# Nineteen table loads split between a GpSimd gather of 120 rows and a ScalarE load of 8, with short gathers between them

## The chip, the cores and the metric

The kernel runs on one core of one Trainium2 chip. The metric is device time in microseconds of one execution; lower is better. A core has TensorE (PE, its weight loads shown apart as PEld), VectorE (DVE), ScalarE (ACT), GpSimd (POOL) and SyncE (SP), which only issues transfers here. Transfers between HBM and the core's memory are carried out by 16 DMA engines; SP, ScalarE and GpSimd each put transfers in a queue of their own, and all queues are served by the same 16 engines.

## The reference

A table of N = 100001 items with D = 128 numbers each, 1024 sequences of T = 50 item numbers, and a spiking unit per sequence and dimension:

```python
e = emb[seq]                                  # 1024 x 50 x 128, row 0 of emb is zero
uF = cumsum(e, axis=1) / min(t, lengths)
y = (uF - mean) * rsqrt(var + BN_EPS) * gamma + beta     # mean, var over the sequences
# scan over t: v += (x - v) / 2; spike = v >= 1; v -= spike
uF_out = spikes.mean(axis=0)                  # 1024 x 128
scores = uF_out @ emb.T                       # 1024 x 100001
```

The output is 1024 x 100001 numbers of 4 bytes, 409.6 MB. The table is 51.2 MB.

## The kernel before, in words

**First stage** (to about 500 us). For each of 50 time steps GpSimd gathers 1024 rows of the table in eight indirect transfers of 128 rows (L208, one short in eight steps, in which SP loads 128 single rows instead, L229). TensorE transposes and sums them, VectorE and ScalarE do the statistics and the spiking step. Meanwhile the first 40 of 98 parts of the table are loaded by SP.

**Second stage.** The table is cut in 98 parts of 1024 rows. A part is loaded as 128 partitions of 8 rows, 4 KB each. The 98 parts are worked off in column groups c of `WIDTHS` parts: four of 2, four of 3, thirteen of 6. Before a group is needed, each of its parts is prepared (`prepare`, L149): TensorE transposes it in eight pieces (L137), ScalarE copies the result into one half of a pair, VectorE the remainder into the other (L153, L154). Then for each of 8 blocks n of 128 output rows (sequences) and each part q of the group, TensorE multiplies (`product`, L161), and ScalarE and VectorE in turn evict the 128 x 1024 result into the block's buffer `o` (L553, L555). When a block's parts are all in, SP stores it (`store`, L170): 128 rows of 24 KB for a group of six, 3 MB. From c = 8 on three `o` buffers take turns, so a block's first eviction waits until the store of three blocks before has landed, on all DMA engines that carry it.

**Loads in the second stage.** Parts 40 to 97 are fetched from c = 8 on, three parts at a time, after the blocks n = 1 and n = 4 of a group (end of the loop over blocks, `fetch(r, k, to_fetch, GROUP // 2)`, L575). `fetch` (L104) issues from ScalarE's queue for these parts: one transfer of 128 partitions x 3 parts x 4 KB. There are 19 of these; the last call fetches what is left, 84 rows of 4 KB and a row of 512 B. Two buffers `rows` of six parts alternate; a part's place is free when its transposes are done. The order of instructions is the order of the program, engine by engine; nothing reorders it.

GpSimd has nothing to do in the second stage, and the indirect gathers of the first stage are its last transfers.

Of the kernel before, what the change touches and what calls it, by code (L numbers as in the profile page):

```python
# [12 lines left out]
F32 = mybir.dt.float32  # L13
BF16 = mybir.dt.bfloat16
F32R = mybir.dt.float32r
I32 = mybir.dt.int32
U32 = mybir.dt.uint32
# [4 lines left out]
P = 128  # L22
BN_EPS = 1e-5
V_TH = 1.0
HALF = 1024
KQ = HALF // P
# [8 lines left out]

BY_SYNC = (11, 17, 22, 28, 33, 38, 43, 48)
AT_ONCE = 32

WIDTHS = 4 * [2] + 4 * [3] + 13 * [6]
NARROW, MIDDLE = 4, 8  # L40
# [3 lines left out]
def rec_kernel(  # L44
# [9 lines left out]
    nc = tc.nc  # L54
    B, T = seq.shape
    N, D = table.shape
# [7 lines left out]
    const = ctx.enter_context(tc.tile_pool(name="const", bufs=1))  # L64
# [9 lines left out]
    held_rows = const.tile([P, BANK], F32, tag="countB", name="held_rows")  # L74
    ids = const.tile([P, B - BANK - P], F32, tag="countC", name="ids")
    ident = const.tile([P, P], F32, tag="ident", name="ident")

# [11 lines left out]
    def size(q):  # L91
        return min(HALF, N - q * HALF)
# [4 lines left out]
    def group(g):  # L97
        at = g if g < AHEAD else AHEAD - 2 + g % 2
        r = rowp.tile([P, GROUP, HALF], F32, tag=f"rows{at}", name=f"rows_{g}")
        for k in range(GROUP):  # L100
            rows[g * GROUP + SHIFT + k if g else k + ASIDE * (k >= TWICE)] = r[:, k, :]
        return r

    def fetch(r, k, q, n):  # L104

        engine = nc.sync if q < held else nc.scalar
        n = min(n, parts - q)
        whole = n - (size(q + n - 1) < HALF)
        if whole:
            engine.dma_start(  # L110
                out=r[:, k : k + whole, :],
                in_=table[q * HALF : (q + whole) * HALF, :].rearrange("(q p k) d -> p q (k d)", p=P, k=KQ),
            )
        if whole < n:
            full, rest = divmod(size(parts - 1), KQ)
            c1 = (parts - 1) * HALF
            r = r[:, k + whole, :]
            if rest:
                at = full - full % 32
                nc.vector.memset(r[at : at + 32, :], 0.0)  # L120
                engine.dma_start(
                    out=r[full : full + 1, : rest * D],
                    in_=table[c1 + full * KQ : N, :].rearrange("(o k) d -> o (k d)", o=1),
                )
            if full:
                engine.dma_start(
                    out=r[:full, :],
                    in_=table[c1 : c1 + full * KQ, :].rearrange("(p k) d -> p (k d)", k=KQ),
                )
# [43 lines left out]
    with ExitStack() as ph:  # L173
# [16 lines left out]
        nc.sync.dma_start(out=gb[:, 1:2], in_=beta.rearrange("(d o) -> d o", o=1))  # L190
        first = group(0)
        fetch(first, 0, 0, TWICE)
        spare = asidep.tile([P, ASIDE, HALF], F32, tag="aside", name="spare")
        for k in range(ASIDE):
            rows[TWICE + k] = spare[:, k, :]
        fetch(spare, 0, TWICE, ASIDE)
        fetch(first, TWICE, SHIFT, GROUP - TWICE)
        for g in range(1, AHEAD):
            fetch(group(g), 0, g * GROUP + SHIFT, GROUP)
# [17 lines left out]
        starts = ids[:T, :P].bitcast(I32)  # L217
        regs = [nc.sync.alloc_register(f"row{k}") for k in range(AT_ONCE)]
        singles = {}

        def fetch_singles(i):
            t = BY_SYNC[i]
            rows_of = held_rows[:, i % (BANK // P) * P :][:, :P]
            singles[t] = rows_of
            for p0 in range(0, P, AT_ONCE):
                nc.sync.load(regs, starts[t : t + 1, p0 : p0 + AT_ONCE])
                for k, reg in enumerate(regs):
# [90 lines left out]
        def over(t, v):  # L318

            d = lp.tile([P, B], BF16, tag="d", name=f"d_{t}")  # L320
            nc.scalar.activation(d, v, AF.Identity, bias=less)  # L321
            return d
# [7 lines left out]
        whole = slice(0, B)  # L330
# [13 lines left out]
        for t in range(T):  # L344
# [29 lines left out]
            r = sp.tile([P, 1], F32, tag="r", name=f"r_{t}")  # L374
# [14 lines left out]
            q = sp.tile([P, 1], F32, tag="q", name=f"q_{t}")  # L389
# [20 lines left out]
            if not last:  # L410
# [12 lines left out]
                d = over(t, v)  # L423
# [3 lines left out]
                if t in (T - 8, T - 6):  # L427
                    q = (t - T + 8) // 2
                    pair(q)
                    prepare(q, vp.tile([P, HALF], F32, tag="v0", name=f"pt_{q}"))  # L430
                    if q == TWICE - 1:
                        for k in range(TWICE):
                            rows[GROUP + ASIDE + k] = first[:, k, :]
                        nc.sync.dma_start(
                            out=first[:, :TWICE, :],
                            in_=table[(GROUP + ASIDE) * HALF : (GROUP + SHIFT) * HALF, :].rearrange(
                                "(q p k) d -> p q (k d)", p=P, k=KQ
                            ),
# [41 lines left out]

    psum = ctx.enter_context(
        tc.tile_pool(name="psum", bufs=4, space=bass.MemoryType.PSUM, reuse_waits="tile")
    )
# [12 lines left out]
    for c, W in enumerate(WIDTHS):  # L498
# [38 lines left out]
        for n, q in blockwise:  # L537
            if n not in os:
                pool, tag, most = turns[blocks % len(turns)]
# [30 lines left out]
            if n in (1, 4) and c >= MIDDLE and to_fetch < parts:  # L570
                g, k = divmod(to_fetch - SHIFT, GROUP)
                if k or to_split >= (g - 1) * GROUP + SHIFT:
                    if k == 0:
                        r = group(g)
# [23 lines left out]
```

## Time and profile before

| what | value |
|---|---|
| median of 3 runs | 1562.74 us (1562.43 to 1562.77) |
| profiled execution, its own time | 1562.34 us |
| its span, first to last instruction | 1560.6 us |
| busy: PE, DVE, ACT, POOL | 1124.4, 949.3, 674.1, 372.8 us |
| written to HBM, read from HBM | 409.60 MB, 77.69 MB |
| DMA queue q1 (SP): packets, MB, share of 16 engines | 32944, 431.39, 65.8% |
| DMA queue q10 (ScalarE) | 7700, 30.23, 4.8% |
| DMA queue q0 (GpSimd) | 12544, 25.72, 6.2% |

How to read it: the page cuts the span in 40 slices of 39 us and gives each engine's busy share in tenths; the line DMA is the mean busy share of the 16 DMA engines. A window `A:B` gives, for a stretch of the span, the busy time of each engine with its instructions in brackets, then the granted TensorE clock, the mean busy share of the 16 DMA engines (0.06 is one engine of sixteen) and the GB/s that they moved. A packet is booked with its whole size at its place, so that shares of full stretches come out up to 1% over 1.00. In lists of waits, "A <- B" says that A's engine stood idle until B.

### The profile page before, as it was taken

The page shows a single profiled execution, that of the slowest core. Times are in us where ns is not written, and L with a number is a line of the kernel's source. Part 1 is how long each engine was busy: PE and PEld are TensorE (multiplying, and loading weights), DVE is VectorE, ACT ScalarE, POOL GpSimd, SP SyncE. Part 2 cuts the span into 40 slices and gives each one's busy share as a digit, 9 for nine tenths or more (in the row PEclk, how much of TensorE's full clock was granted, in tenths as well). Part 3 has the DMA queues.
Part 4 walks back from the last instruction along what each step waited for, and adds up shares of the span by engine and source line. Part 5 has one row for each costly group of instructions (what it writes and reads, how often), then busy time and mean ns, then how long its engine had stood idle before and what let it go on. Part 6 is the DMA issues. An engine that isn't in the chain of part 4 may idle for free.

```text
span 1560.6 us, 14364 instructions
## 1 busy us (share of the span) xinstructions
PE 1124.4 (72%) x4465; PEld 802.4 (51%) x4465; DVE 949.3 (61%) x1128; ACT 674.1 (43%) x698; POOL 372.8 (24%) x398
## 2 busy tenths in 40 slices
PE   4444444444445989989878888788887878888884
PEld 2211211111133777768666666666666656666663
DVE  5777777777778665667555555455555445555552
ACT  2333333333344555555444444444444444444442
POOL 7777777777775000000000000000000000000000
PEclk9999999999996999999999999989999999999997
DMA  9722222222223999999999999999999999999998
GB/s 346 270 54 54 54 55 54 54 54 54 54 55 106 402 407 417 420 413 405 426 427 427 420 427 424 429 408 416 426 428 427 418 425 403 433 416 426 429 386 364
DMA packets 53265, 488.25 MB, mean 313 GB/s; under 512 B 10991, under 2 KB 12272, under 8 KB 32068
## 3 DMA queue, kind: packets, MB, share of 16 engines
q1 hardware_dynamic: 32944, 431.39, 65.8%
q0 software_dynamic: 12544, 25.72, 6.2%
q10 hardware_dynamic: 7700, 30.23, 4.8%
q8 instruction: 35, 0.57, 0.1%
q14 instruction: 42, 0.34, 0.1%
HBM read 77.69 MB, written 409.60 MB: 312 GB/s over the span
## 4 chain that ended last, share of the span: by engine, by line
DMA 46%; POOL 20%; PE 14%; issue 10%; DVE 4%; ACT 4%; ACTq 0%; POOLq 0%; SPq 0%; DVEq 0%
DMA scores<-o 44%; POOL e L208 20%; PE po L161 13%; DVE o L553 3%; ACT o L555 3%; DMA e<-in_L_rec_emb_table,idx 2%; DVE pairs L154 1%; ACT pairs L153 1%; PE pt L137 0%; ACT hi L153 0%; PE pre L351 0%; DVE lo L154 0%; PE warm L337 0%; DMA idx<-in_r_seq 0%; ACTq L555 0%
## 5 line engine op out<-in xcount | busy, mean ns | idle before, releaser
L553 DVE TENSOR_SCALAR o<-po 128x1024 f32<-128x1024 f32 (+1 forms) x390 | 466.7, 1214 | 324.8 <-DMA scores<-o 184.5
L555 ACT ACTIVATE o<-po 128x1024 f32<-128x1024 f32 x392 | 392.9, 1025 | 498.4 <-DMA scores<-o 367.9
L208 POOL DMA_INDIRECT e<-in_L_rec_emb_table,idx x392 | 372.1, 949 | 121.5 <-issue 116.5
L161 PE MATMUL po<-pairs,countB 128*128 128x512 f32 (+1 forms) x1120 | 292.9, 408 | 59.1 <-ACT o L555 59.1
L351 PE MATMUL pre<-ident,e 128*128 128x128 f32 x392 | 171.9, 461 | 216.0 <-DMA e<-in_L_rec_emb_table,idx 214.7
L161 PE MATMUL po<-pairs,countC 128*128 128x512 f32 (+1 forms) x840 | 239.9, 433 | 58.1 <-ACT o L555 51.2
L161 PEld LDWEIGHTS po<-pairs,countB 128*128 128x128 f32 x1120 | 211.7, 194 | 120.6 <-ACT o L555 78.1
L351 PEld LDWEIGHTS pre<-ident,e 128*128 128x128 f32 x392 | 72.2, 185 | 318.6 <-DMA e<-in_L_rec_emb_table,idx 317.8
L161 PEld LDWEIGHTS po<-pairs,countC 128*128 128x128 f32 x840 | 169.1, 209 | 110.2 <-ACT o L555 62.5
L154 DVE TENSOR_TENSOR pairs<-pt,pairs 128x1024 fp32r<-128x1024 f32 x70 | 85.3, 1218 | 96.3 <-ACT pairs L153 96.2
L362 DVE SCALAR_TENSOR_TENSOR uF<-rlen,pre 128x512 f32<-128x512 f32 x100 | 68.3, 683 | 97.8 <-PE pre L351 97.7
L137 PE MATMUL pt<-ident,rows 128*128 128x128 f32 (+1 forms) x768 | 105.2, 282 | 10.0 <-DVE rows L134 4.9
L137 PEld LDWEIGHTS pt<-ident,rows 128*128 128x128 f32 (+1 forms) x768 | 94.7, 147 | 27.2 <-issue 10.8
L375 ACT ACTIVATE r<-mv,eps 128x1 f32<-128x1 f32 x50 | 14.8, 295 | 209.8 <-DVE mv L371 209.8
L309 PE MATMUL pre<-zT,ls 128*128 128x512 f32 x100 | 77.6, 778 | 26.2 <-DVE uF L362 22.3
L161 PE MATMUL po<-hi,countB 128*128 128x512 f32 x208 | 84.9, 408 | 13.4 <-ACT o L555 11.8
L153 ACT CAST pairs<-pt 128x1024 fp32r<-128x1024 f32 x70 | 70.1, 1014 | 41.3 <-PE pt L137 41.3
L161 PE MATMUL po<-lo,countB 128*128 128x512 f32 x208 | 83.0, 399 | 0.0
L321 ACT ACTIVATE d<-v,less 128x1024 bf16<-128x1024 f32 x49 | 54.5, 1113 | 65.4 <-DVE v L408 62.3
L161 PE MATMUL po<-hi,countC 128*128 128x512 f32 x156 | 67.7, 434 | 13.6 <-ACT o L555 12.4
L405 ACT ACTIVATE v<-uF,hgb,a 128x1024 f32<-128x1024 f32 x49 | 59.2, 1208 | 30.6 <-DVE a L401 30.6
L363 DVE BATCH_NORM_STATS2 bs<-uF 128x6 f32<-128x512 f32 x100 | 69.4, 694 | 3.4
(94 smaller groups left out, 858.5 us busy)
## 6 DMA issues: line engine op xcount, KB each, us to landing
scores<-o SPq DMA_DIRECT2D x96, 3072.0 KB
scores<-o SPq DMA_DIRECT2D x32, 1536.0 KB
scores<-o SPq DMA_DIRECT2D x29, 1024.0 KB
rows<-in_L_rec_emb_table ACTq DMA_DIRECT2D x19, 1536.0 KB
scores<-o SPq DMA_DIRECT2D x8, 2896.5 KB
held_rows<-in_L_rec_emb_table SPq DMA_DIRECT2D x1024, 0.5 KB
rows<-in_L_rec_emb_table SPq DMA_DIRECT2D x5, 3072.0 KB
e<-in_L_rec_emb_table,idx POOLq DMA_INDIRECT x392, 2.6
```

The lines of the kernel that those rows point to most:

```text
L137: nc.tensor.transpose(pt[:, k0 : k0 + pw], r[:pw, k0 : k0 + D], ident[:pw, :pw])
L153: nc.scalar.copy(vh, vp)
L154: nc.vector.tensor_tensor(vl, vp, vh.bitcast(F32), ALU.subtract)
L161: nc.tensor.matmul(po[:, :kw], lhsT=counts[n], rhs=part[:, k0 : k0 + kw], start=j == 0, stop=j == 1,)
L208: nc.gpsimd.indirect_dma_start(out=es[t][:, n * P : (n + 1) * P], out_offset=None, in_=table, in_offset=bass.IndirectOffsetOnAxis(ap=idx[: ...
L309: nc.tensor.matmul(pre[h], lhsT=l, rhs=zT[:, h * BANK : (h + 1) * BANK], start=t == 0, stop=False, skip_group_check=True,)
L351: nc.tensor.matmul(pre[h][:, k : k + P], lhsT=singles[t] if h * BANK + k + P == B and t in singles else e[:, h * BANK + k : h * BANK + k + P],
L362: nc.vector.scalar_tensor_tensor(uF[:, cs], rlen[:, cs], 1.0 / (t + 1), pre[h], ALU.max, ALU.mult)
L363: nc.vector.bn_stats(bs[:, h, :], uF[:, cs])
L405: nc.scalar.activation(vt, uF[:, cs], AF.Identity, bias=hgb[:, 1:2], scale=a)
L553: nc.vector.tensor_scalar_mul(o[:, h0 : h0 + hw], po[:, :hw], 1.0 / T)
L555: nc.scalar.mul(o[:, h0 : h0 + hw], po[:, :hw], 1.0 / T)
```

## The change

Of each of the 19 three-part loads, the third part (parts 42, 45, ... 96) is no longer in ScalarE's transfer, which now takes 128 partitions x 2 parts. The third part comes in two transfers: GpSimd gathers its first 120 rows of 4 KB (partitions 0 to 119) by an indirect transfer whose row numbers stand in a small table `picks`, made once by an `iota`; ScalarE loads its last 8 rows (partitions 120 to 127) by a plain transfer. After each such gather GpSimd issues a short one, `turn_by(17)`: 17 elements of 8 bytes into a tile that nothing reads. Before the second stage a single `turn_by(5)` gathers 5 such elements. The bytes of the table that arrive, and all arithmetic, are the same.

```diff
+SPARED = 120
+PICKED = range(42, 97, 3)
+TURN = 17
...
+    runs = table[: N // KQ * KQ, :].rearrange("(n k) d -> n (k d)", k=KQ)
+
+    def turn_by(m):
+        nc.gpsimd.indirect_dma_start(
+            out=turned_by[:m, :],
+            out_offset=None,
+            in_=table.rearrange("n (k d) -> (n k) d", d=2),
+            in_offset=bass.IndirectOffsetOnAxis(ap=picks[:m, 0:1].bitcast(U32), axis=0),
+        )
+
+    def pick(r, q, engine):
+        j = PICKED.index(q)
+        nc.gpsimd.indirect_dma_start(
+            out=r[:SPARED, :],
+            out_offset=None,
+            in_=runs,
+            in_offset=bass.IndirectOffsetOnAxis(ap=picks[:SPARED, j : j + 1].bitcast(U32), axis=0),
+        )
+        engine.dma_start(out=r[SPARED:, :], in_=runs[q * P + SPARED : (q + 1) * P, :])
+        turn_by(TURN)
+
     def fetch(r, k, q, n):
 
         engine = nc.sync if q < held else nc.scalar
         n = min(n, parts - q)
         whole = n - (size(q + n - 1) < HALF)
-        if whole:
+        wide = whole - (whole == n and q + whole - 1 in PICKED)
+        if wide:
             engine.dma_start(
-                out=r[:, k : k + whole, :],
-                in_=table[q * HALF : (q + whole) * HALF, :].rearrange("(q p k) d -> p q (k d)", p=P, k=KQ),
+                out=r[:, k : k + wide, :],
+                in_=table[q * HALF : (q + wide) * HALF, :].rearrange("(q p k) d -> p q (k d)", p=P, k=KQ),
             )
+        if wide < whole:
+            pick(r[:, k + wide, :], q + wide, engine)
...
+    nc.gpsimd.iota(picks, pattern=[[PICKED.step * P, len(PICKED)]], base=PICKED.start * P, channel_multiplier=1)
+    turn_by(5)
```

More of the change, by code (lines that the diff above doesn't have):

```diff
@@ L76, in rec_kernel @@
     ident = const.tile([P, P], F32, tag="ident", name="ident")
+    picks = const.tile([P, len(PICKED)], I32, tag="picks", name="picks")
+    turned_by = const.tile([TURN, 2], F32, tag="turned_by", name="turned_by")
     parts = -(-N // HALF)
```

## The prediction

> **What bounds the kernel now.** I read the page's parts 2, 3 and 6 first, then windows over the stage of stores, then what waits in it.
>
> ```profile
> PE   4444444444445989989878888788887878888884
> DMA  9722222222223999999999999999999999999998
> ...
> q1 hardware_dynamic: 32944, 431.39, 65.8%
> q0 software_dynamic: 12544, 25.72, 6.2%
> q10 hardware_dynamic: 7700, 30.23, 4.8%
> ...
> rows<-in_L_rec_emb_table ACTq DMA_DIRECT2D x19, 1536.0 KB
> ```
>
> From slice 13 on (about 500 us) the 16 DMA engines are full while TensorE is not. q1 carries the stores, q10 ScalarE's loads, q0 GpSimd's gathers, which all lie in the first stage. So the second stage is priced in time of DMA engines. The windows below cut it at the places where the DMA share falls (columns after the engines' busy times: granted clock, DMA share, GB/s).
>
> ```profile
> 795.50:888.50 93.00, 73.26 (x321) 57.32 (x322) 48.60 (x41) 41.27 (x42) 0.00 (x0) 0.93 1.01 429
> 888.50:891.50 3.00, 3.00 (x14) 2.47 (x13) 2.02 (x2) 1.03 (x1) 0.00 (x0) 0.94 0.65 276
> 891.50:1022.80 131.30, 108.96 (x471) 85.58 (x470) 69.92 (x60) 58.69 (x59) 0.00 (x0) 0.92 1.01 427
> 1022.80:1025.80 3.00, 3.00 (x15) 2.47 (x14) 2.39 (x2) 1.32 (x2) 0.00 (x0) 1.00 0.48 205
> 1025.80:1090.30 64.50, 52.41 (x228) 41.03 (x227) 33.57 (x29) 28.43 (x29) 0.00 (x0) 0.92 1.01 430
> 1090.30:1093.30 3.00, 3.00 (x15) 2.45 (x14) 2.19 (x2) 1.08 (x2) 0.00 (x0) 1.00 0.48 205
> 1093.30:1224.50 131.20, 109.33 (x472) 86.08 (x471) 70.29 (x60) 58.44 (x59) 0.00 (x0) 0.92 1.01 427
> 1224.50:1227.50 3.00, 3.00 (x15) 2.49 (x14) 1.96 (x2) 1.80 (x2) 0.00 (x0) 1.00 0.78 330
> 1227.50:1291.50 64.00, 51.14 (x222) 39.84 (x221) 33.45 (x28) 27.06 (x29) 0.00 (x0) 0.92 1.01 427
> 1291.50:1295.50 4.00, 4.00 (x18) 3.23 (x18) 2.33 (x2) 2.22 (x3) 0.00 (x0) 0.98 0.41 172
> 1295.50:1487.40 191.90, 160.01 (x703) 125.47 (x703) 106.04 (x90) 86.86 (x88) 0.00 (x0) 0.93 1.01 426
> 1487.40:1492.40 5.00, 5.00 (x19) 4.06 (x18) 2.17 (x3) 2.05 (x2) 0.00 (x0) 0.78 0.30 121
> 1492.40:1554.60 62.20, 42.22 (x181) 33.22 (x179) 25.16 (x24) 22.94 (x23) 0.00 (x0) 0.89 1.00 425
> 1554.60:1559.20 4.60, 0.00 (x0) 0.00 (x0) 0.00 (x0) 0.00 (x0) 0.00 (x0) 0.50 0.09 35
> ```
>
> Six short stops and a tail, and between them full engines. The stops lose 3.0x0.35 + 3.0x0.52 + 3.0x0.52 + 3.0x0.22 + 4.0x0.59 + 5.0x0.70 = 10.7 us of all 16 engines, the tail 4.6x0.91 = 4.2 us. Who still works in them?
>
> ```profile
> 1489.95:1491.40 1.45, 1.45 (x8) 1.17 (x7) 0.96 (x1) 0.71 (x1) 0.00 (x0) 1.00 0.04 17
> 1555.40:1556.30 0.90, 0.00 (x0) 0.00 (x0) 0.00 (x0) 0.00 (x0) 0.00 (x0) 0.50 0.12 51
> 1556.50:1559.10 2.60, 0.00 (x0) 0.00 (x0) 0.00 (x0) 0.00 (x0) 0.00 (x0) 0.50 0.06 27
> ```
>
> A share of 0.06 at 27 GB/s is one engine of sixteen at its full pace (q1: 431.39 MB in 65.8% of 16 x 1560.6 us is 26 GB/s an engine). So one engine is last by 4.4 us at the end, and at most one works in the middle of a stop. That it is the same engine throughout is my reading; the views do not name engines. It fits what the consumers wait for: a buffer is free when the last engine has landed its rows.
>
> ```profile
> 1477.87 18.30 SPq L170 DMA_DIRECT2D scores<-o  x3
> 1480.91 1.02 ACT L555 ACTIVATE o<-po 128x1024 f32<-128x1024 f32 x1 [4.21 <-DMA scores<-o]
> ...
> ACT o L555 <- DMA scores<-o: 281.2, 83, 6.4
> ```
>
> ScalarE waits 281.2 us of 765 for landings. Before the stop of 1487 it got its buffer only at 1480.9, and the block that it then evicted reached the queue too late for fifteen engines. On this reading the late engine never rests and sets the stage; the others stand idle 10.7x16/15 = 11.4 us in the stops and 4.2x16/15 = 4.5 us at the end: **15.9 us**, the most that moving work off it can return.
>
> **The change, part by part.** *Which engines.* What a transfer of few rows does must be inferred.
>
> ```profile
> DMA packets 307, 4.67 MB, mean 425 GB/s; under 512 B 46, under 2 KB 47, under 8 KB 131
> ...
> q10 hardware_dynamic: 100, 0.34, 7.7%
> ```
>
> This is 1443 to 1454 us, the last load: 84 rows of 4 KB and one of 512 B. The 19 whole loads take the other 7600 packets, 400 each: 384 rows and 16 completions. The last one's 100 packets are 85 rows and so 15 completions: one for the single row, 14 for the 84. So 84 rows went to 14 engines, the greatest number up to 16 that divides 84. If gathers divide alike (in the trace they have 128 rows only: 12544/392 = 32 packets, 16 of them data), 120 rows go to 15 engines of 8 rows, 17 to one, 5 to five, and ScalarE's 8 to eight. If each gather starts where the one before ended, 15 + 1 = 16 brings the turn back, so the same engine is left out nineteen times. [...]
>
> *Price of a row.* q10: 4.8% of 16 x 1560.6 us over 30.23 MB gives 0.162 us for 4 KB. The spared engine loses 19x8x0.162 = 24.7 us. If it is one of the eight that take the last rows it gets 3.1 us back; the seven others of the eight get +3.1 us each.
>
> *Gathered rows against loaded ones.* The filled stretch 0 to 70 us has both:
>
> ```profile
> q1 hardware_dynamic: 5750, 20.21, 77.4%
> q0 software_dynamic: 1632, 3.35, 13.6%
> ```
>
> 866.9 us for 20.21 MB is 0.176 us per 4 KB on q1; 152.3 us for 3.35 MB is 0.186 on q0, 6% more. Over the whole page q0 has 0.247, most of it from a stage whose engines are nearly empty. For 152 rows an engine the surplus is 0.01x152 = 1.5 us (bounds: 0, and (0.247-0.162)x152 = 12.9). I take 1.5, since the second stage is full as 0 to 70 is.
>
> *Short gathers.* Seventeen 8-byte elements on one engine, nineteen times. The nearest row is the single rows of the first stage, 100 to 430 us:
>
> ```profile
> q1 hardware_dynamic: 1640, 0.42, 0.5%
> ...
> held_rows<-in_L_rec_emb_table SPq DMA_DIRECT2D x822, 0.5 KB
> ```
>
> 26.4 us for 822 rows of 512 B, 0.032 us each; 17x0.032x19 = 10.3 us above, nothing below; I take half, 5.2 us, and on the engine that the turn ends on, the spared one.
>
> *Issue.* The order shows where they stand. On GpSimd after its last gather of the first stage (e is that stage's tile, rows the loaded one); before:
>
> ```order
> L208 DMA e_3277<-in_L_rec_emb_table,idx 128x128 x7
> L208 DMA e_3319<-in_L_rec_emb_table,idx 128x128 x8
> L594 UNCONDITIONAL_BRANCH
> L594 ISA
> ```
>
> and now:
>
> ```order
> L238 DMA e_3321<-in_L_rec_emb_table,idx 128x128 x8
> L513 IOTA picks 128x19
> L113 DMA turned_by<-in_L_rec_emb_table,picks 5x2
> L122 DMA rows_5442<-in_L_rec_emb_table,picks 120x1024
> L113 DMA turned_by<-in_L_rec_emb_table,picks 17x2
> L122 DMA rows_5442<-in_L_rec_emb_table,picks 120x1024
> ```
>
> GpSimd waits only for its own buffers. On ScalarE, at the first load, before:
>
> ```order
> L153 CAST pairs_4329<-pt_5427 128x1024
> L110 DMA rows_5438<-in_L_rec_emb_table 128x3x1024
> L555 ACTIVATE o_5_5440<-po_26_5441 128x1024
> ```
>
> and now:
>
> ```order
> L183 CAST pairs_4333<-pt_5431 128x1024
> L138 DMA rows_5442<-in_L_rec_emb_table 128x2x1024
> L128 DMA rows_5442<-in_L_rec_emb_table 8x1024
> L588 ACTIVATE o_5_5447<-po_26_5448 128x1024
> ```
>
> One load becomes two.
>
> ```profile
> L110 ACTq DMA_DIRECT2D rows<-in_L_rec_emb_table x19: 374/374/428, 791.8 to 1398.7; - x19
> 493.96 0.94 POOL L208 DMA_INDIRECT e<-in_L_rec_emb_table,idx  x1 [0.30 <-issue]
> ```
>
> 19x0.374 = 7.1 us of ScalarE's queue, ahead of evictions, covered by the 281.2 us that it waits for landings; without that cover it would cost 7.1 us. GpSimd issues 39 gathers at 0.94 + 0.30, 48 us, on an engine with nothing else after 495 us. The rows that land are read late: the load of 791.8 us is transposed two groups of blocks on, after 891, so a gather that is some us late holds nobody.
>
> *Sum*, against the profiled run (span 1560.6, its time 1562.34 us; the median of the runs is 1562.74). The late engine: -24.7 + 3.1 + 5.2 = -16.4 us, more than enough to stop being last. An ordinary engine of the eight: -15.9 (its idle time goes) + 3.1 + 1.5 = -11.3 us. The tail's row 1555.4 with share 0.12 shows a second engine late by 1.5 us, which then ends last: -9.8 us. 1562.34 - 9.8 + 0.4 = **1552.9 us**. TensorE, 109 busy of 131 us, has room for 1% more pace.
>
> **Rivals.**
> (a) *The turn stands wrong, and the late engine gets more.* It is not the spared one but among the eight: +3.1 for last rows, +1.5 for dearer rows, 1562.7 + 4.6 = 1567.3 us. It decides as soon as the spared engine is another. For it: no view names an engine. Against: nothing in the trace. [...]
> (b) *Wrong engine, not among the eight*: only the dearer rows, 1564.2 us. No change that can be told.
> (c) *Gathered rows cost what the page's mean says*: 15.9 - 3.1 - 12.9 - 1.5 = -1.6, so 1564.3 us. For it: 0.247 on q0. Against: the full stretch's 0.186.
> (d) *Half the relief*: the spared engine's stores slow down while the others load, or the stops have a share of block boundaries in them that the late engine did not cause (they come about every 67 or 134 us, where a group of blocks ends and its transposes stand). 8.2 us of relief, less the 3.1 that loads others meanwhile: about 5 us, 1557.7.
>
> **How the numbers follow.** Forecast 0.58 (own range 1549 to 1556: relief down to 11.3 still suffices, dearer rows or a second late engine take 3, none gives 3), (d) 0.10, (b) 0.13, (c) 0.07, (a) 0.12. A measurement of this kernel tells about 0.2%, 3.1 us, from no change: forecast and (d) are faster, 0.68; (b) and (c) same, with a little of (a), 0.21; the rest slower, 0.11. The range for 8 in 10 runs from 1549.5 to 1565.5 us: it takes in (b), (c) and (d) and leaves out (a) and the forecast's lower end.
>
> **What would show it.** Right: the stops at 889, 1023, 1091, 1225, 1292 and 1488 shrink below half in the DMA share; the tail with one engine goes under 2.5 us; ScalarE's 281 us for landings falls; q0 gains 19x120 packets of 4 KB at 0.16 to 0.19 us. Wrong engine: stops and tail as before with the share of q0 there. Dear rows: no stops, no tail, and yet the same time, with q0's price near 0.25. The forecast fails if the late engine is only late by chance of the run, or if the stops come from the transposes at the boundaries.

## The result, and the profile after

The changed kernel takes 1550.06 us (median, 1549.26 to 1551.55) against 1562.88 us: ratio 0.9918, 95% interval 0.9905 to 0.9931, 12.8 us less. 1552.9 us had been forecast. Its profiled execution took 1549.26 us with a span of 1547.4 us, 13.2 us less than before.

The same windows as in the prediction, on the changed kernel (granted clock, DMA share and GB/s stand last):

```profile
795.50:888.50 93.00, 77.67 (x337) 60.85 (x336) 51.42 (x43) 43.06 (x44) 5.28 (x5) 0.93 1.01 427
888.50:891.50 3.00, 3.00 (x15) 2.41 (x14) 1.79 (x2) 1.69 (x2) 0.00 (x0) 1.00 1.04 442
891.50:1022.80 131.30, 109.96 (x465) 85.74 (x464) 69.31 (x59) 57.62 (x58) 8.35 (x8) 0.91 1.00 427
1022.80:1025.80 3.00, 3.00 (x14) 2.44 (x13) 1.98 (x2) 1.71 (x2) 0.00 (x0) 1.00 1.07 459
...
1090.30:1093.30 3.00, 3.00 (x14) 2.45 (x13) 1.74 (x2) 1.23 (x2) 0.00 (x0) 1.00 1.01 434
...
1224.50:1227.50 3.00, 3.00 (x14) 2.42 (x13) 2.21 (x2) 1.47 (x2) 0.00 (x0) 1.00 0.96 410
...
1291.50:1295.50 4.00, 4.00 (x18) 3.03 (x17) 2.43 (x3) 2.31 (x3) 0.00 (x0) 1.00 0.99 424
1295.50:1480.00 184.50, 157.16 (x690) 122.65 (x688) 103.77 (x87) 85.13 (x87) 6.26 (x6) 0.94 1.01 427
1480.00:1490.00 10.00, 10.00 (x47) 8.17 (x46) 5.42 (x6) 4.87 (x5) 0.00 (x0) 1.00 1.01 429
1490.00:1541.00 51.00, 31.18 (x134) 23.62 (x132) 19.29 (x18) 17.80 (x18) 0.00 (x0) 0.91 1.00 428
1541.00:1545.70 4.70, 0.00 (x0) 0.00 (x0) 0.00 (x0) 0.00 (x0) 0.00 (x0) 0.50 0.47 202
```

Where the DMA share had fallen to 0.30 to 0.78 it is 0.96 to 1.07 now, also around 1484, where the last of these stops should have moved to. All 10.7 us of the stops are gone. The tail is still 4.7 us long but of another kind: it loses 4.7x0.53 = 2.5 us of all engines instead of 4.2, and engine after engine ends in it, where one had run alone:

```profile
1541.00:1543.00 2.00, 0.00 (x0) 0.00 (x0) 0.00 (x0) 0.00 (x0) 0.00 (x0) 0.50 0.76 324
1543.00:1544.00 1.00, 0.00 (x0) 0.00 (x0) 0.00 (x0) 0.00 (x0) 0.00 (x0) 0.50 0.49 209
1544.00:1545.70 1.70, 0.00 (x0) 0.00 (x0) 0.00 (x0) 0.00 (x0) 0.00 (x0) 0.50 0.13 55
```

10.7 + 4.2 - 2.5 = 12.4 us of idle time recovered, out of 13.2 us of span. ScalarE's waits in this stage:

```profile
POOL rows L122 <- PE pt L167: 424.9, 9, 49.8
ACT o L588 <- DMA scores<-o: 236.8, 68, 6.2
```

ScalarE waits 236.8 us for landings instead of 281.2. GpSimd waits long for its buffers (the transposes of the part that was there before), as it should: in the whole second stage the trace puts one wait of ScalarE, 3.0 us, down to a gather.

### The profile page after: what moved, and what is told of

Read it like the earlier page. It is cut to its first block, busy times and chain, and to the rows that moved or that the text cites. A ratio compares the mean times of both kernels' runs of the same rounds, so it can differ in the third digit from the quotient of the medians.

```text
span 1547.4 us, 14481 instructions
## 1 busy us (share of the span) xinstructions
PE 1129.9 (73%) x4465; PEld 802.7 (52%) x4465; DVE 949.2 (61%) x1128; ACT 674.5 (44%) x698; POOL 413.7 (27%) x438
## 3 DMA queue, kind: packets, MB, share of 16 engines
q10 hardware_dynamic: 5572, 20.89, 3.3%
## 4 chain that ended last, share of the span: by engine, by line
DMA 41%; PE 20%; POOL 19%; issue 10%; DVE 6%; ACT 4%; ACTq 0%; SPq 0%; DVEq 0%; POOLq 0%
DMA scores<-o 38%; PE po L191 19%; POOL e L238 19%; DVE o L586 3%; ACT o L588 3%; DMA e<-in_L_rec_emb_table,idx 3%; DVE pairs L184 1%; PE pt L167 1%; ACT pairs L183 1%; DVE lo L184 0%; ACT hi L183 0%; DVE bs L393 0%; DVE uF L392 0%; PE pre L381 0%; DVE negv L355 0%
## 5 line engine op out<-in xcount | busy, mean ns | idle before, releaser
L122 POOL DMA_INDIRECT rows<-in_L_rec_emb_table,picks x19 | 18.6, 978 | 716.0 <-PE pt L167 713.2
```

## The experiments

A pick is below one part of the table that is loaded by a gather of 120 rows and a load of the last 8. Two theories. **A**: one DMA engine is late throughout the second stage, and the gain comes from leaving out exactly that one. **B**: the gain comes from a third queue, from smaller transfers on ScalarE's queue or from an earlier issue by GpSimd, whichever engine is left out.

**e1_turn6: the turn one further.**

```diff
-    turn_by(5)
+    turn_by(6)
```

> The changed kernel with six instead of five elements in the first short gather, so that every gather of 120 rows stands one engine further on. Theory A (one engine is late in all of the second stage, and the gain comes from leaving out exactly that one): the late engine keeps its 8 rows and may get a ninth, so the gain is gone: 1562.9 us of before plus 0 to 4.6, that is 1562.5 to 1567.5 us, with stops and a one-engine tail of over 4 us as before. Theory B (the gain comes from a third queue, from smaller transfers on ScalarE's queue or from an earlier issue by GpSimd, whichever engine is left out): as the changed kernel, 1549 to 1551.5 us.

Measured 1567.83 us (1567.43 to 1568.95) against 1562.74: ratio 1.0033 (1.0022 to 1.0045). One element of 8 bytes more in one transfer, and the whole gain is gone and 5.1 us more. The stops are back, and the one-engine tail (share 0.05 over 3 us):

```profile
1094.00:1098.00 4.00, 4.00 (x17) 3.21 (x16) 1.97 (x2) 1.80 (x2) 0.00 (x0) 0.86 0.43 184
1493.00:1497.50 4.50, 4.50 (x18) 3.58 (x17) 2.12 (x2) 2.05 (x2) 0.00 (x0) 0.83 0.36 151
1561.00:1564.00 3.00, 0.00 (x0) 0.00 (x0) 0.00 (x0) 0.00 (x0) 0.00 (x0) 0.50 0.05 23
```

B falls here. The measured time is 0.3 us above A's range, whose upper end is the case in which the late engine takes a ninth row. The packet records of the trace, which the next section explains, show that case: in the loads from 1335 to 1403 us the late engine takes its rows of the gather and one of ScalarE's last eight.

**e2_no_turn: gathers of 120 rows, no short ones**, so that the engine left out moves on.

```diff
-        turn_by(TURN)
...
-    turn_by(5)
```

> The changed kernel without any short gather: each gather of 120 rows starts where the one before ended, so that another engine is left out each time. Theory A: the late engine is left out once or twice of nineteen, 7 to 16 rows at 0.162 us, 1.1 to 2.6 us, less up to 1.5 us for dearer rows: 1560 to 1564 us. Theory B: 1549 to 1551.5 us, or a little less because the short gathers are gone.

1565.67 us (1565.30 to 1567.16), ratio 1.0021 (1.0011 to 1.0030): no gain, against B, and 1.7 us beyond A's range. What the expectation left out are the last eight rows, 3.1 us if the late engine is among the eight that take them; with them, added after the result, A gives 1563 to 1567. The stops and the lone engine at the end are there:

```profile
957.50:962.00 4.50, 4.50 (x17) 3.57 (x16) 1.89 (x2) 2.05 (x2) 0.00 (x0) 0.77 0.46 189
1557.00:1561.70 4.70, 0.00 (x0) 0.00 (x0) 0.00 (x0) 0.00 (x0) 0.00 (x0) 0.50 0.07 30
```

**e3_all128: the gather takes all 128 rows.**

```diff
-SPARED = 120
+SPARED = 128
...
-        engine.dma_start(out=r[SPARED:, :], in_=runs[q * P + SPARED : (q + 1) * P, :])
-        turn_by(TURN)
...
-    turn_by(5)
```

> The third part of each load comes from GpSimd as one gather of all 128 rows; ScalarE loads no last 8, no short gathers. No engine is left out. Theory A: only the price of gathered rows shows, 152 rows an engine at 0 to 0.01 us dearer: 1562.5 to 1565 us; at the page's mean of 0.247 us a row it would be 1575 us. Theory B: 1549 to 1552 us.

1563.40 us, ratio 1.0005 (0.9996 to 1.0015). GpSimd's queue by itself does nothing that can be told, good or bad. There are stops as in the kernel before, and the lone engine at the end:

```profile
1025.00:1028.00 3.00, 3.00 (x14) 2.44 (x13) 1.95 (x2) 1.54 (x2) 0.00 (x0) 1.00 0.42 180
1429.00:1432.50 3.50, 3.50 (x14) 2.77 (x14) 1.76 (x2) 1.15 (x2) 0.00 (x0) 0.81 0.38 162
1556.50:1560.00 3.50, 0.00 (x0) 0.00 (x0) 0.00 (x0) 0.00 (x0) 0.00 (x0) 0.50 0.06 26
```

**e4_half: ten picks instead of nineteen.**

```diff
-PICKED = range(42, 97, 3)
+PICKED = range(42, 97, 6)
```

> Ten picks instead of nineteen (every second load's third part). Theory A: the late engine loses 70 rows, 11.3 us, less at most 2.7 us for short gathers, and is last again by a few us: a gain of 8.5 to 11.4 us, 1551.5 to 1554.5 us, with a one-engine tail back. Theory B: the gain goes with the number of gathers, 10/19 of 12.8 us: 1556 us.

1554.14 us, ratio 0.9947 (0.9930 to 0.9963): 8.6 us, at the lower edge of A's 8.5 to 11.4 and more than the 6.7 us of 10/19. The late engine is last again:

```profile
1420.50:1422.50 2.00, 2.00 (x10) 1.61 (x9) 1.35 (x2) 1.03 (x1) 0.00 (x0) 1.00 0.75 320
1481.00:1484.00 3.00, 3.00 (x13) 2.38 (x13) 2.19 (x2) 1.06 (x2) 0.00 (x0) 0.97 0.55 227
1548.00:1550.40 2.40, 0.00 (x0) 0.00 (x0) 0.00 (x0) 0.00 (x0) 0.00 (x0) 0.50 0.05 19
```

Only two stops, late in the stage, and a lone engine for some 4 us: it needs a large part of the stage to fall behind again.

The next four kernels ran twice. The first time the kernel before took 1859.07 us beside them, its first stage being some 300 us longer; a few us can't be told there, so the second time counts.

**e5_double: the second part of each load is gathered too, 38 picks.**

```diff
-PICKED = range(42, 97, 3)
+PICKED = [q for q in range(41, 97) if q % 3 != 1]
...
-        wide = whole - (whole == n and q + whole - 1 in PICKED)
+        wide = whole - 2 * (whole == n and q + whole - 1 in PICKED)
...
-            pick(r[:, k + wide, :], q + wide, engine)
+            for j in range(wide, whole):
+                pick(r[:, k + j, :], q + j, engine)
...
-    nc.gpsimd.iota(picks, pattern=[[PICKED.step * P, len(PICKED)]], base=PICKED.start * P, channel_multiplier=1)
+    nc.gpsimd.iota(picks, pattern=[[3 * P, len(PICKED) // 2], [P, 2]], base=PICKED[0] * P, channel_multiplier=1)
```

> The second part of each load is gathered and split in the same way as the third: 38 picks. Theory A: the spared engine now loses some 40 us and rests; the seven others of the lowest eight get another 19 rows, 3.1 us, and dearer gathered rows, 0 to 1.5 us: 1550.1 + 3.1 + 0 to 1.5 = 1553 to 1555 us. Theory B (more gathers, more gain): below 1549 us.

> The same kernel as e5_double: 38 picks. In the first look the stage from the first 24 KB store took 846.7 us, 10.6 more than the changed kernel's 836.1 and 3.3 less than before's 850.0: so 1558 to 1561 us, instead of the 1553 to 1555 of theory A, which would leave some 5 us that the ninth rows of the lowest eight engines and the surplus of gathered rows don't explain. If the first look was disturbed: 1553 to 1555 us.

First 1859.34 against 1859.07 (0.9983 to 1.0023); then 1561.37 us against 1562.76, ratio 0.9990 (0.9980 to 0.9999). So more picks give 11.3 us back. B's further gain is refuted a second time, but theory A with its prices (1553 to 1555) misses by 6 us. The queues of the whole page, first of the changed kernel (span 1547.4), then of this one (span 1558.8):

```profile
q1 hardware_dynamic: 32944, 431.39, 66.0%
q0 software_dynamic: 15920, 35.08, 7.9%
q10 hardware_dynamic: 5572, 20.89, 3.3%
```

```profile
q1 hardware_dynamic: 32944, 431.39, 66.1%
q0 software_dynamic: 19264, 44.44, 9.1%
q10 hardware_dynamic: 3444, 11.55, 1.8%
```

On SP's queue, which carries the stores and the first stage's loads, the mean engine spends 0.661x1558.8 = 1030 us instead of 0.660x1547.4 = 1021 us on the same bytes; loads and gathers on the other two queues together cost 3.4 us less. The 24 KB rows of the stores, 768 an engine, take 928 ns in the mean of the packet records instead of 919, 7 us of these 9. No idle time came back. From 795 to 1540 us the engines are as full as in the changed kernel and move less, first the changed kernel, then this one:

```profile
795.00:1540.00 745.00, 620.77 (x2676) 484.38 (x2674) 400.44 (x337) 334.00 (x336) 36.57 (x35) 0.93 1.01 428
795.00:1540.00 745.00, 618.40 (x2682) 479.81 (x2680) 399.75 (x337) 332.97 (x336) 75.90 (x73) 0.95 1.01 423
```

Why a store's row takes longer with 38 picks stays open.

**e6_low4 and e6_low5: which engine is it?** The kernel before, without gathers; ScalarE loads the third part in four pieces. In e6_low5 the line `CUTS` has (96, 22, 5, 5); the rest is the same.

```diff
+CUTS = (96, 24, 4, 4)
...
+        cut = CUTS if engine is nc.scalar and whole == n else ()
+        wide = whole - (1 if cut else 0)
+        if wide:
...
+        p0 = 0
+        for m in cut:
+            r0 = (q + wide) * HALF + p0 * KQ
+            engine.dma_start(
+                out=r[p0 : p0 + m, k + wide, :],
+                in_=table[r0 : r0 + m * KQ, :].rearrange("(p k) d -> p (k d)", k=KQ),
+            )
+            p0 += m
```

> The kernel before, no gathers. ScalarE loads the third part of each of the 19 loads in four transfers of 96, 24, 4 and 4 rows. [...] Theory A with the late engine being number 4 (the one that five, fifteen and a turn from 0 leave out): its load is unchanged, the four that get 2x19x0.162 = 6.2 us more have 15.9 us of idle time: 1562 to 1564.5 us. [...]

> The same kernel as e6_low4, beside a kernel before of 1562 us (beside the first one the first stage took 300 us longer, in the kernel before too, and blurred a few us). [...] From the first look, the stage from the first 24 KB store on took 855.9 us, against 850.0 in the kernel before elsewhere. Theory A with late engine 4: 1562 to 1566 us (the small transfers on ScalarE's queue may cost some). Late engine among 0 to 3: 1568 to 1571 us.

> [...] Theory A with the late engine being number 4: 6.2 us more on it, 1568 to 1570.5 us. [...]

> The same kernel as e6_low5. Theory A with late engine 4: 6.2 us more than the run with 4 and 4 rows. If it is another engine: within 1.5 us of that run. The first looks differed by 2.7 us, between the two.

First 1867.35 (ratio 1.0052, 1.0030 to 1.0074) and 1870.75 (1.0054, 1.0035 to 1.0073); then 1569.67 us (1.0040, 1.0027 to 1.0054) and 1571.59 us (1.0053, 1.0037 to 1.0068). Both lose 7 to 9 us and differ by 2, neither the 0 nor the 6.2 that would name the engine by the time. The pieces themselves cost too much. Of e6_low4_b, ScalarE's queue on the page, and its issues of the third part:

```profile
q10 hardware_dynamic: 8384, 30.23, 5.4%
```

```profile
L120 ACTq DMA_DIRECT2D rows<-in_L_rec_emb_table x76: 261/1068/1794, 792.0 to 1404.8; - x76
```

The same 30.23 MB take 5.4% of 1564.9 us of the mean engine instead of 4.8% of 1560.6: 84.5 us instead of 74.9. And 76 issues at a median of 1.07 us stand in front of evictions, 81 us of ScalarE's queue beside the 7 of the whole loads. Which of the two costs the time stays open. Which pieces the late engine carries does not: the packet records of the last ten loads (next section) show it. In e6_low5_b it takes the rows of the 96 and the 22 and one row of each piece of five (nine loads), in e6_low4_b those of the 96 and the 24 and none of the pieces of four (seven loads; in the others it can't be followed). So it is the engine that a piece of five has and a piece of four has not. The expectations call it number 4 and those of a piece of four 0 to 3: the numbers are the author's names, the records have none, and on which engines the other pieces fall is not shown.

**e7_upper: the last eight rows on either half.** In ten of the nineteen picks GpSimd gathers them, after a short gather that is meant to turn to the other eight engines; on which eight they fell is not shown.

```diff
-        engine.dma_start(out=r[SPARED:, :], in_=runs[q * P + SPARED : (q + 1) * P, :])
-        turn_by(TURN)
+        if j % 2:
+            engine.dma_start(out=r[SPARED:, :], in_=runs[q * P + SPARED : (q + 1) * P, :])
+            turn_by(TURN)
+            return
+        turn_by(4)
+        nc.gpsimd.indirect_dma_start(
+            out=r[SPARED:, :],
+            out_offset=None,
+            in_=runs,
+            in_offset=bass.IndirectOffsetOnAxis(ap=lasts[:, j : j + 1].bitcast(U32), axis=0),
+        )
+        turn_by(5)
...
+    nc.gpsimd.iota(lasts, pattern=[[PICKED.step * P, len(PICKED)]], base=PICKED.start * P + SPARED, channel_multiplier=1)
```

> The changed kernel, but in ten of the nineteen picks the last 8 rows are gathered by GpSimd on the upper eight engines (short gathers of 4 and 5 elements bring the turn there and back), so that the last rows weigh 1.5 us on either half instead of 3.1 us on the lower. Theory A: the end comes with the mean of the engines, 1 to 1.6 us earlier: 1548.5 to 1549.5 us. If the end is set by something else than the lower eight engines: 1550 us or, with more gathers to issue, later.

> The same kernel as e7_upper: last rows on either half of the engines in turn. Theory A: 1548.5 to 1549.5 us. The first look's stage from the first 24 KB store took 838.0 us against the changed kernel's 836.1: by that 1550 to 1552 us, no gain.

First 1846.24 against 1859.07, ratio 0.9939 (0.9918 to 0.9959); then 1551.54 us, ratio 0.9927 (0.9913 to 0.9940). No gain over the changed kernel, whose interval (0.9905 to 0.9931) overlaps: the attempt to spread the last rows, with its further transfers, gains nothing, against theory A's 1548.5 to 1549.5. No version tried beats the changed kernel.

## Why the prediction was right, point by point

**One late engine, and the others' idle time as the most to be had (15.9 us).** Shown: with the one turn that helps, stops and lone tail vanish; with the turn one further (e1), with a moving turn (e2) or with no engine left out (e3) they are there.

The trace also shows what makes the engine late. Its packet records have start and duration of each packet, but no engine. On a full engine the next packet starts 3 or 4 ns before the end of the one before it, so the sixteen chains of packets can be followed, except where two would fit. In the stage of 24 KB rows, cut in 23 stretches of 30 us from 800 us on, one chain of the kernel before has a median of 927 ns or more a row in each stretch, and no other is above 919. With nineteen picks one chain gets none of the gathered rows; it holds the packet of 136 B of the short gather:

```
rows of 24 KB of                             rows   median ns
before, the slowest chain of each stretch     661         935
before, the other fifteen                    9937         912
after, the slowest chain of each stretch      675         938
after, the chain without gathered rows        115         944
e4_half, the chain without gathered rows       37         942
e1_turn6, the chain without gathered rows      65         912
e1_turn6, the slowest chain of each stretch   657         936
```

So the change leaves out the slow engine, and e1 leaves out an ordinary one, while the slow one works on. The engine is as slow in the changed kernel as before, only no longer last: it ends at 1544.9 us, the sixteen between 1541.5 and 1545.7. 768 rows of 24 KB at 14 ns (by the means, 935 and 921) to 23 ns (by the medians) more make it 11 to 18 us late, an estimate which has the 15.9 us of idle time in it. Why its rows take longer no run shows.

**The same engine nineteen times, by 15 + 1 = 16.** Shown by e1 and e2 together: the turn is set by the short gathers, it stays where it is put, and it matters to one step (1550.06 us with five elements in the first short gather, 1567.83 with six, 1565.67 without short gathers). The packet records of the changed kernel show the 120 rows as 8 on each of fifteen engines, and the 17 elements in one packet of 136 B on the sixteenth, nineteen times; the five elements before them are five packets of 8 B. ScalarE's two transfers of a load leave 24 packets of 4 B, sixteen and eight; in the nine loads in which the chain that holds the 136 B can be followed past them, it has two of them. So the engine left out is one of the eight that take the last rows. That all eight are the same in every load, which the 3.1 us for an ordinary engine need, was the author's assumption and no run shows it. Nor does any run show an engine's number, or on which one the first gather starts. Rival (a) fell; e1 is what it would have looked like, 1567.8 us where (a) gave 1567.3.

**The size was off by 3 us (9.8 forecast, 12.8 measured)**, by two terms of the sum. First, "152 rows an engine at 0.01 us", 1.5 us for dearer gathered rows: there is none. In the second stage of the changed kernel, 795 to 1480 us:

```profile
q1 hardware_dynamic: 12020, 262.65, 89.7%
q10 hardware_dynamic: 5572, 20.89, 7.5%
q0 software_dynamic: 3252, 9.02, 3.3%
```

7.5% of 16 x 685 us over 20.89 MB is 0.161 us per 4 KB on ScalarE's queue; 3.3% over 9.02 MB is 0.164 on GpSimd's, short gathers included. And e3, with all rows gathered, is 0.7 us slower with an interval from -0.6 to 2.3, which can't exclude the 1.5 us by itself. The 0.186 taken from the start of the kernel was for rows of 512 B, eight to a packet; the page's 0.247 (rival c), most of it from the first stage, had no bearing. Second, "the tail's row shows a second engine late by 1.5 us, which then ends last": no such 1.5 us were lost. In the packet records of the kernel before its chain runs with the others up to 1520 us; then a packet of 16 KB on the queue "instruction" (0.88 us, from 1526.64 us) stands in it, and from there on it ends each store 1.7 to 1.9 us after most of them. In the changed kernel the last such packet came at 1511.31 us, and three engines end within 0.4 us of each other. Without the two terms the sum is 15.9 - 3.1 = 12.8 us, what was measured. That it fits so exactly is in part luck: that the 3.1 us of the last rows are what is missing from 15.9 was not shown, as e7, which was meant to halve them on each engine, gains nothing.

**Short gathers, 5.2 us.** Too high, and harmless. The trace's packet records of the changed kernel show for the nineteen of them, from 790 us on:

```
size    packets   mean us each
136 B        19   0.025
 68 B       285   0.026
```

that is one packet of 17 x 8 B and fifteen of 68 B for each: at most 0.026 us on every engine, 0.5 us in all nineteen.

**ScalarE's second load, 0.374 us each, covered.** It is longer than that, and still covered by the 236.8 us that ScalarE waits for landings: the load of 8 rows takes 1.34 us to issue where the one of 128 partitions takes 0.39, 25 us of ScalarE's queue.

```profile
L138 ACTq DMA_DIRECT2D rows<-in_L_rec_emb_table x19: 385/385/435, 792.1 to 1388.9; - x19
L128 ACTq DMA_DIRECT2D rows<-in_L_rec_emb_table x19: 1177/1341/1662, 792.5 to 1389.4; - x19
```

**(d), half the relief, or stops that belong to the group boundaries.** All stops go with the late engine; with it relieved, the DMA share at the boundaries is 0.96 to 1.07. That they lay at the boundaries because the transposes there use up the slack that the late engine had left is a reading that no run tests.

## What to carry to other kernels

When a stage is full of transfers and still has short dips, look at who works in the dips: here a DMA share of 0.06 at the end, at 27 GB/s, was one engine that came late, and the time that the others stand idle is the most that can be had. Here rows taken off that engine paid, and rows taken off its neighbour paid nothing and cost their detour, so a run with the turn one step further belongs beside such a change. The dose has to be found: ten picks gave 8.6 us, nineteen 12.8, thirty-eight 1.4. By the idle time alone, 15.9 us at 8 x 0.162 us a pick, twelve would have been enough, an estimate that leaves out what the other engines take on; no run has twelve.

## What had not been expected of the hardware

One DMA engine took 2.5% longer for a row of 24 KB than the fifteen others (935 against 912 ns), through the stage of 24 KB stores; it is 935 to 938 against 912 in all six kernels whose chains were followed, before, after and e1 to e4. A load of 8 rows took 1.34 us to issue from ScalarE, one of 256 rows 0.39 us. Loads whose third part was cut in pieces of 96, 24, 4 and 4 rows cost the mean engine 84.5 us instead of 74.9 for the same bytes. SP's queue cost it 9 us more when twice as many loads left an engine out (e5). And the first stage's single-row loads by SP, 0.40 us apart in the kernel before, were 0.72 us apart in the first run of e6_low4, whose first stage, like that of the kernels beside it, took some 300 us longer. First of the kernel before, then of e6_low4, SyncE's timeline:

```profile
300.00 80.08 SPq L229 DMA_DIRECT2D held_rows<-in_L_rec_emb_table  x201
```

```profile
380.64 79.48 SPq L240 DMA_DIRECT2D held_rows<-in_L_rec_emb_table  x110
```
